# State space beside attention: softplus of all four channel parts ahead of the products, two parts at a time, and the rows of B and C in a pool of their own

## The chip, the core and the metric

The kernel runs on one core of a Trainium2 chip. Five engines with their own instruction queues work beside each other: TensorE (PE in the profile, its weight loads are PEld), VectorE (DVE), ScalarE (ACT), GpSimd (POOL) and SyncE (SP), which here issues nearly all DMAs. Each engine takes its instructions in the order of its queue, and waits at the first whose inputs or buffers are not ready, whatever stands behind it. The metric is the device time of one execution in microseconds, the median of the runs.

## What is computed

One sequence of four sublayers over `x` of shape (2, 1024, 256), each with a residual: attention with 16 heads of 128 and ALiBi, a ternary-quantized feed-forward layer, a selective state space (Mamba) layer, and a feed-forward layer that keeps two of four. The change is in the third:

```python
xz = einsum('bld,ed->ble', hidden_states, in_proj_weight);  x, z = split(xz)
x_conv = silu(sum(xp[:, w:w+l, :] * conv1d_weight[:, w] for w in range(4)))
x_dbl = einsum('bld,ed->ble', x_conv, x_proj_weight)   # dt_low (128), B (16), C (16)
delta = softplus(einsum('blr,dr->bld', dt_low, dt_proj_weight) + dt_proj_bias)
deltaA = exp(einsum('bld,dn->lbdn', delta, A))          # A = -exp(A_log)
dBu = einsum('bld,bln,bld->lbdn', delta, Bm, x_conv)
h = deltaA * h + dBu;  y = einsum('bdn,bn->bd', h, c)   # a scan over l
y = (y + x_conv * D) * silu(z);  out = einsum('bld,ed->ble', y, out_proj_weight)
```

There are 512 channels, held as four channel parts of 128 partitions, and 16 states: 64 pairs (part c, state n), called products below. `delta` is the softplus that the change moves. All is float32 here.

## The kernel before

The 2 x 1024 positions are cut into four chunks of 512: chunk 0 and 1 are the halves of the first sequence, 2 and 3 those of the second. Attention of a chunk is 16 heads of four tiles (128 queries each); a head of a second half sees 1024 keys and costs more than one of a first half. The loop at the end of the program runs attention of chunk k = 1, 2, 3 as a generator, and beside it, as another generator `rest(k-1)`, the other three sublayers of the chunk before. The first chunk's attention runs ahead of it, with the quantization of weights, and `rest(3)` runs alone at the end, the tail.

How the two are interleaved is written out: after each attention tile, `rest` is advanced until the sum of what it yielded has reached its share of `cost(k)`. A product yields 2.2 units, a softplus step 3. So a yield decides beside which attention tile, and so where in each engine's queue, the instructions behind it stand. Scans also carry an order against attention's row sums (`pace["front"]`, L756).

`state_space(k)` has a front and the products. **Front:** layernorm; input projection (L608); convolution on DVE (L624, L626); silu; the low-rank part `dtl` (matmul L639, copied to SBUF); softplus of part 0 by `steps(0)`; then B and C (`bcp` matmul, L648), stored to DRAM (L658), from where every product loads its row, broadcast to 128 partitions.

`steps(c)` (L544 to L575) is softplus of one part, 512 wide: a matmul into a PSUM bank of `ps_r` (L547, `dt`); on ACT Abs (L555, `se`), Relu (L556, `sv`), Exp (L561) and Ln (L563, `dl`); on DVE a correction `sr` (L568, L569); on POOL `dl` + `sr` (L570), plus `sv` (L572; on DVE where `short`, that is for chunk 1), and times `xs` (L574, `du`). `sv` and `se` have one buffer, `dl` and `du` two. steps(1), steps(2), steps(3) stand in the middle of the products of the part before, after product 16c - 8.

**Products.** Each of the 64 runs through stages with lags, in a software pipeline: ask for the rows of B and C (`bs`, `cs`, L691, SP's DMA queue, rings of 5 and 4 buffers), `db` = `du` x B (L736, POOL), `da` = exp(A x `dl`) (L750, ACT, into a bank of `ps_r`, of which there are two), the scan `hs` (L757, DVE), keep the last column (L766, DVE), `hc` = `hs` x C (L771, POOL), and the sum over n as transposes added in PSUM (`y`, L701, PE). At the end of a part the gate (L786 to L793). In the tail `db` comes from PE and ACT, and the buffers are more.

Attention, beside this, has scores on PE (`s`, L362), mask, ALiBi and row minimum on DVE (L366, L372), the exponential on ACT (L377), transposes on PE (`pt`, L293) copied to SBUF (`pT`, L296, ACT or DVE), `z` (L304, copied as `zs`, L309), the output product (`o`, L318) added to `x` on DVE (L324), and for the next head `pq`, `pk` (L335), `pv` (L342) on PE with their copies `qT`, `kT` (L338) and `v` (L347) on ACT, the last on ACT or DVE.

The memory pools matter too. The front's weights and activations (`mi`) are closed before the products' pool `m2` opens in their place, so the first row loads and buffers of `m2` wait until the front's last readers are done.

Of the kernel before, what the change touches and what calls it, by code (L numbers as in the profile page):

```python
# [9 lines left out]
F32 = mybir.dt.float32  # L10
BF16 = mybir.dt.bfloat16
F32R = mybir.dt.float32r
AF = mybir.ActivationFunctionType
ALU = mybir.AluOpType
# [3 lines left out]
P = 128  # L18
# [8 lines left out]
DI, DN, DR, DC = 512, 16, 128, 4  # L27
NDC = DI // P
NX = DR + 2 * DN
U = 512  # L30
# [11 lines left out]
def kernel(  # L42
# [21 lines left out]
    nc = tc.nc  # L64
# [6 lines left out]
    def bank(tag, bufs):  # L71
        return lambda name, dt=F32: ps.tile([P, 512], dt, tag=tag, name=name, bufs=bufs)
# [3 lines left out]
    ps_y, ps_r = bank("y", 1), bank("r", 2)  # L76
# [156 lines left out]
    for h in range(H):  # L233
# [10 lines left out]
    rows = a2.tile([H, S], F32, tag="alibi", name="rows", padded_shape=[P, S])  # L244
    nc.gpsimd.iota(
        rows, pattern=[[1, S]], base=0, channel_multiplier=0, allow_small_or_imprecise_dtypes=True,
# [179 lines left out]
    dt_bias = lambda c: cols_sb[:, c, DC + DN : DC + DN + 1]  # L426
# [90 lines left out]
    def state_space(k):  # L517
        b, u = CH[k]
        first, last, tail_end = u == 0, u == NU - 1, k == len(CH) - 1
        ps_da = ps_s if tail_end else ps_r  # L520

        short = not tail_end and CH[k + 1][1] == 0
        with ExitStack() as mctx:
            mc = mctx.enter_context(tc.tile_pool(name="mc", bufs=1, side="right"))
            dt_sb = mc.tile([P, DI], F32, name=f"dt_sb_{k}")
            out_sb = mc.tile([P, NDC, D], F32, name=f"out_sb_{k}")
            xs = mc.tile([P, NDC, U], F32, name=f"xs_{k}")
            sz = mc.tile([P, NDC, U], F32, name=f"sz_{k}")
            dtl = mc.tile([P, U], F32, name=f"dtls_{k}")
            work = lambda name: mc.tile([P, U], F32, tag="cv", name=name, bufs=2)  # L530
            diag = mc.tile([P, DN, UT, P], F32, name=f"diag_{k}") if tail_end else None
            one = mc.tile([P, 1], F32, name=f"one_{k}")
# [8 lines left out]
            marks = []  # L541
            paced = not tail_end

            def steps(c):  # L544

                vp = ps_r(f"dt_{k}_{c}")
                ended["by"] = nc.tensor.matmul(  # L547
                    vp, lhsT=dt_sb[:, c * P : (c + 1) * P], rhs=dtl, start=True, stop=True
                )


                v = row_of("sv", f"sv_{k}_{c}", 1)
                e = row_of("se", f"se_{k}_{c}", 1)
                with tc.issue_after(marks[0].ins):
                    nc.scalar.activation(e, vp, AF.Abs, bias=dt_bias(c))  # L555
                relu = lambda: nc.scalar.activation(v, vp, AF.Relu, bias=dt_bias(c))  # L556

                idle = tail_end and c == 0
                if not idle:
                    relu()  # L560
                nc.scalar.activation(e, e, AF.Exp, scale=-1.0)  # L561
                l = row_of("dl", f"dl_{k}_{c}", 2)
                log = nc.scalar.activation(l, e, AF.Ln, bias=one)  # L563
                if idle:
                    with tc.issue_after(log.ins):
                        relu()
                r = work(f"sr_{k}_{c}")
                nc.vector.tensor_scalar(r, e, 1.0, -1.0, ALU.add, ALU.add)  # L568
                marks.append(nc.vector.tensor_tensor(r, e, r, ALU.subtract))  # L569
                (nc.vector if idle else nc.gpsimd).tensor_tensor(l, l, r, ALU.add)  # L570
                dl = l
                (nc.vector if short or idle else nc.gpsimd).tensor_tensor(dl, v, l, ALU.add)  # L572
                du = row_of("du", f"du_{k}_{c}", 2)
                marks.append((nc.vector if idle else nc.gpsimd).tensor_tensor(du, dl, xs[:, c, :], ALU.mult))  # L574
                return dl, du  # L575

            def turned(c, du):

                tp = ps_r(f"dup_{k}_{c}")
                for t in range(UT):  # L580
                    nc.tensor.transpose(
                        tp[:, t * P : (t + 1) * P], du[:, t * P : (t + 1) * P], ident
                    )
                duT = row_of("duT", f"duT_{k}_{c}", 2)
                nc.scalar.copy(duT, tp)
                return duT


            with ExitStack() as ictx:

                mi = (mctx if tail_end else ictx).enter_context(tc.tile_pool(name="mi", bufs=1, side="right"))
                if tail_end:
                    in_sb = carried["in"]
                else:
                    in_sb = mi.tile([P, KC, 2 * DI], F32, name=f"in_sb_{k}")
                    nc.sync.dma_start(out=in_sb, in_=inT.rearrange("(c p) m -> p c m", p=P))
                xp_sb = mi.tile([P, NDC, NX], F32, name=f"xp_sb_{k}")
                nc.sync.dma_start(out=xp_sb, in_=xpT.rearrange("(c p) m -> p c m", p=P))
                nc.sync.dma_start(out=dt_sb, in_=dtT)
                nc.sync.dma_start(out=out_sb, in_=outT.rearrange("(c p) m -> p c m", p=P))  # L600
# [37 lines left out]
                for c in range(NDC):  # L638
                    nc.tensor.matmul(  # L639
                        dl_ps, lhsT=xp_sb[:, c, :DR], rhs=xs[:, c, :],  # L640
                        start=(c == 0), stop=(c == NDC - 1),
                    )
                nc.any.tensor_copy(dtl, dl_ps)
                parts, turns = {0: steps(0)}, {}
                yield 3
                bc_ps = ps_da(f"bcp_{k}")
                for c in range(NDC):
                    last_bc = nc.tensor.matmul(  # L648
                        bc_ps[: 2 * DN, :], lhsT=xp_sb[:, c, DR:], rhs=xs[:, c, :],
                        start=(c == 0), stop=(c == NDC - 1),  # L650
                    )
                if tail_end:
                    ended["by"] = last_bc
                    fill_in()
                bc = mi.tile([2 * DN, U], F32, name=f"bc_{k}", padded_shape=[P, U])
                nc.any.tensor_copy(bc, bc_ps[: 2 * DN, :])

                nc.sync.dma_start(out=bcd.rearrange("a n t -> (a n) t"), in_=bc)  # L658
                if tail_end:
# [7 lines left out]
                    bT = mc.tile([P, UT, DN], F32, name=f"bTs_{k}")  # L667
                    nc.vector.tensor_copy(bT, bT_ps[:, :, :DN])
                yield 4

            m2 = mctx.enter_context(tc.tile_pool(name="m2", bufs=1, side="right"))
            part = lambda tag, name, bufs: m2.tile([P, U], F32, tag=tag, name=name, bufs=bufs)
# [12 lines left out]
            def row(rows, a, tag, bufs):  # L685
                def ask(i):
                    c, n = prods[i]
                    if a == 0 and by_tensor(i):
                        return
                    rows[i] = part(tag, f"{tag}_{k}_{c}_{n}", bufs)  # L690
                    nc.sync.dma_start(  # L691
                        out=rows[i], in_=bcd[a, n : n + 1, :].to_broadcast([P, U])
                    )
                return ask
# [105 lines left out]
            for i in range(-5, len(prods) + DRAIN(k)):  # L800
                for lag, f in stages:
                    if 0 <= i - lag < len(prods):
                        f(i - lag)
                if i >= 0:
                    yield 2.2
                if 0 <= i < len(prods) and i // DN + 1 < NDC:
                    c = i // DN + 1
                    if i % DN == (DN // 4 if tail_end else DN // 2):
                        parts[c] = steps(c)
                        yield 3  # L810
                    if tail_end and i % DN == DN - 5:
                        turns[c] = turned(c, parts[c][1])
            for t in range(UT):
                op = (spare(k) if t % 2 else ps_r)(f"mo_{k}_{t}")
                for c in range(NDC):
                    ended["by"] = nc.tensor.matmul(  # L816
                        op[:, :D], lhsT=xs[:, c, t * P : (t + 1) * P], rhs=out_sb[:, c, :],
                        start=(c == 0), stop=(c == NDC - 1),
# [151 lines left out]
    for k in range(1, len(CH)):  # L970
        r, done = rest(k - 1), 0.0
# [76 lines left out]
```

## Time and profile before

| | us |
|---|---|
| median of 3 runs | 1836.29 (1833.47, 1836.29, 1837.93) |
| span of the profiled execution | 1836.9 |
| first `db` to last `hc`, chunk 0 | 348.47 to 566.27 |
| the same, chunk 1 | 824.43 to 1004.93 |
| the same, chunk 2 | 1237.73 to 1454.35 |

The profiled execution's own time is its span; it lies 0.6 us from the median. Times in the profile are microseconds from the start of the span. A window's row gives the busy time of each engine with the number of instructions, then TensorE's granted clock as a share of full speed, the DMA engines' busy share and GB/s. In a timeline a row gives start, duration, engine, line, operation, names and shape; the bracket holds the time the engine sat idle before it and what ended that. In a groups' row the figures behind the bar are busy time and mean ns, then idle time before the group by what ended it. Line numbers are those of the kernel before.

### The profile page before, as it was taken

The numbers are of one execution on the slowest core, as the hardware profiler recorded it, in microseconds if no ns is written. First come the engines' busy times: TensorE is split into PE (matmuls) and PEld (weight loads), VectorE is DVE, ScalarE is ACT, GpSimd is POOL, SyncE is SP. The second block draws the span as 40 slices with busy tenths as digits, with TensorE's granted clock in tenths as the row PEclk, the third lists the DMA queues.
The fourth block names the chain that finished last, engine by engine and source line by source line (L and its number), as shares of the span: only waits on it lengthen the run. The fifth ranks groups of instructions, "written<-read, shape, count | busy, mean of one in ns | idle before, by whom it ended". The sixth has DMA issues, their size and how long they took to land. (4 is left out here: it accounts for less than half of the span.)

```text
span 1836.9 us, 24217 instructions
## 1 busy us (share of the span) xinstructions
PE 1718.3 (94%) x7956; PEld 1144.2 (62%) x7956; DVE 1218.3 (66%) x2349; ACT 963.7 (52%) x1789; POOL 832.2 (45%) x674
## 2 busy tenths in 40 slices
PE   7999999998999999998888999999999999998899
PEld 4666666555656557755555667756656565566895
DVE  5666555777785473458886565557788655667975
ACT  3444474656563553555554545566555446446742
POOL 3324032588892000419998000418898500035870
PEclk9999999999999999999999999999999999999999
DMA  6443512466662311337787324227665430212541
GB/s 201 128 142 128 193 46 88 149 203 204 216 202 91 103 52 48 125 109 232 245 247 224 116 71 141 82 67 228 226 214 184 142 115 26 75 53 86 178 136 57
DMA packets 178301, 255.99 MB, mean 139 GB/s; under 512 B 16240, under 2 KB 90992, under 8 KB 177152
## 3 DMA queue, kind: packets, MB, share of 16 engines
q1 hardware_dynamic: 176752, 241.61, 41.4%
q0 software_dynamic: 1152, 12.58, 1.9%
q8 instruction: 63, 1.03, 0.2%
q14 instruction: 62, 0.51, 0.1%
q10 hardware_dynamic: 272, 0.26, 0.0%
HBM read 232.04 MB, written 22.35 MB: 138 GB/s over the span
## 5 line engine op out<-in xcount | busy, mean ns | idle before, releaser
L771 POOL TENSOR_TENSOR hc<-hs,cs 128x512 f32<-128x512 f32 x256 | 362.1, 1428 | 10.8 <-DVE ss L366 3.1
L362 PE MATMUL s<-kT,qT 128*128 128x512 f32 (+3 forms) x768 | 302.7, 495 | 19.9 <-DVE ss L366 18.0
L377 ACT ACTIVATE ss<-ss,nm 128x128 f32<-128x128 f32 (+7 forms) x256 | 198.8, 776 | 183.5 <-DVE nm L372 174.1
L366 DVE SCALAR_TENSOR_TENSOR ss<-s,lower 128x512 f32<-128x512 f32 (+3 forms) x384 | 204.6, 549 | 121.0 <-PE s L362 119.4
L736 POOL TENSOR_TENSOR db<-du,bs 128x512 f32<-128x512 f32 x192 | 259.2, 1356 | 44.4 <-DVE hs L757 30.6
L304 PE MATMUL z<-pT,v 128*128 128x512 f32 (+3 forms) x768 | 264.5, 492 | 10.9 <-ACT pT L296 10.2
L372 DVE CUSTOM_DVE_ANT_0 ss<-ss,alibi 128x128 f32<-128x128 f32 (+7 forms) x256 | 241.3, 945 | 3.5
L750 ACT ACTIVATE da<-dl,a_neg 128x512 f32<-128x512 f32 x256 | 177.9, 698 | 115.6 <-DVE hs L757 90.6
L304 PEld LDWEIGHTS z<-pT,v 128*128 128x128 f32 x768 | 142.8, 190 | 145.1 <-issue 92.7
L296 ACT COPY pT<-pt 128x512 f32<-128x512 f32 (+3 forms) x321 | 145.4, 474 | 162.0 <-PE pt L293 160.4
L293 PE MATMUL pt<-ident,ss 128*128 128x128 f32 x1152 | 180.3, 279 | 32.1 <-DVE x L324 18.5
L293 PEld LDWEIGHTS pt<-ident,ss 128*128 128x128 f32 x1152 | 140.0, 142 | 94.7 <-DVE x L324 33.0
L362 PEld LDWEIGHTS s<-kT,qT 128*128 128x128 f32 x768 | 127.9, 193 | 84.1 <-issue 43.4
L757 DVE TENSOR_TENSOR_SCAN hs<-da,db 128x512 f32<-128x512 f32 x128 | 153.8, 1210 | 38.6 <-ACT da L750 20.8
L757 DVE TENSOR_TENSOR_SCAN hs<-da,carry,db 128x512 f32<-128x512 f32 x128 | 159.1, 1269 | 24.4 <-POOL hc L771 14.7
L324 DVE SCALAR_TENSOR_TENSOR x<-o,rr,x 128x256 f32<-128x256 f32 x256 | 108.9, 476 | 76.7 <-PE o L318 76.5
L701 PE MATMUL y<-ident,hc 128*128 128x128 f32 x1024 | 144.8, 279 | 8.4 <-POOL hc L771 8.4
L342 PEld LDWEIGHTS pv<-wv,xT_a 128*128 128x128 f32 x1024 | 124.4, 192 | 37.1 <-issue 25.3
L342 PE MATMUL pv<-wv,xT_a 128*128 128x128 f32 x1024 | 125.8, 275 | 5.5 <-ACT zs L309 3.4
L701 PEld LDWEIGHTS y<-ident,hc 128*128 128x128 f32 x1024 | 121.0, 145 | 14.3 <-POOL hc L771 11.9
L318 PE MATMUL o<-wo,zs 128*128 128x256 f32 x512 | 125.4, 386 | 4.1 <-ACT kT L338 3.0
L335 PE MATMUL pq<-xT_a,wq 128*128 128x512 f32 x256 | 122.7, 601 | 0.7 <-ACT xT_a L148 0.7
(204 smaller groups left out, 2468.7 us busy)
## 6 DMA issues: line engine op xcount, KB each, us to landing
cs<-bcd SPq DMA_DIRECT2D x256, 256.0 KB, 3.8
bs<-bcd SPq DMA_DIRECT2D x192, 256.0 KB, 4.3
alibi<-alibi_d SPq DMA_DIRECT2D x32, 512.0 KB, 4.2
wq<-in_wqT_dram SPq DMA_DIRECT2D x64, 128.0 KB, 3.5
wk<-in_wkT_dram SPq DMA_DIRECT2D x64, 128.0 KB, 3.1
wv<-in_wvT_dram SPq DMA_DIRECT2D x64, 128.0 KB, 2.8
wo<-in_woT_dram SPq DMA_DIRECT2D x64, 128.0 KB, 2.8
alibi<-alibi_d SPq DMA_DIRECT2D x32, 256.0 KB, 3.6
```

Source lines behind the costliest of these rows:

```text
L293: nc.tensor.transpose(tp[:, i, :], s[:, (kb0 + i) * P : (kb0 + i + 1) * P], ident)
L304: nc.tensor.matmul(zp[:, q0:], lhsT=st["v_all"][:, kb, :], rhs=st["pts"][kb // 4][:, kb % 4, q0:], start=(kb == 0), stop=(kb == last),)
L342: nc.tensor.matmul(vp[:, t, :], lhsT=xT[:, c, t * P : (t + 1) * P], rhs=st["v"][:, c, :], start=(c == 0), stop=(c == KC - 1),)
L362: nc.tensor.matmul(sp[:, :n], lhsT=st["qT"][:, j * P : (j + 1) * P], rhs=st["kT"][:, k0 : k0 + n], start=True, stop=True,)
L366: nc.vector.scalar_tensor_tensor(s[:, k0 : k0 + n], sp[:, :n], CLIP, lower[:, S - W + k0 : S - W + k0 + n], op0=ALU.min, op1=ALU.max,)
L372: pace["tile"] = nc.vector.tensor_tensor_reduce(out=s[:, :W], in0=s[:, :W], in1=st["alibi"][:, :W], scale=1.0, scalar=3.0e38, op0=ALU.add, ...
L377: nc.scalar.activation(s[:, :W], s[:, :W], AF.Exp, bias=nm, scale=-1.0, accum_out=st["rs"][:, j : j + 1])
L701: nc.tensor.matmul(yTs[c][:, t * P : (t + 1) * P], lhsT=h[:, t * P : (t + 1) * P], rhs=ident, is_transpose=True, start=start and t == 0, s ...
L736: nc.gpsimd.tensor_tensor(db[i], du, brow.pop(i), ALU.mult)
L750: nc.scalar.activation(da[i], parts[c][0], AF.Exp, scale=a_neg[:, c, n : n + 1])
L757: nc.vector.tensor_tensor_scan(out=hs[i], data0=da.pop(i), data1=db.pop(i), initial=0.0 if first else carry[:, n, c : c + 1], op0=ALU.mult ...
L771: nc.gpsimd.tensor_tensor(hc[i], hs.pop(i), crow.pop(i), ALU.mult)
```

## The change

For chunks 0, 1 and 2 the softplus of all four parts is taken in the front, after B and C are stored and ahead of the products, by a new function `steps_of(pool, a)`: the same operations as `steps`, on two parts at once. The matmul, Abs and Relu stay one part each (a PSUM bank holds 512), Exp, Ln, the correction and the POOL operations take tiles of 2 x 512. It is called for parts 0 and 1 and then for parts 2 and 3; each time a pool `st` with one buffer of `sv`, `se` and `sr` is opened in the same memory, and each call yields 6 units. The results `dls`, `dus` hold all four parts. The mid-product steps and their yields of 3 are left to the tail, which is otherwise as before. `cost` is not changed: 9 units leave the products and the front has 9 more.

The memory is laid out anew: the rows of B and C have a pool `rings` that is open from the front on, instead of a place in `m2`; `dt_sb`, `dtl`, `xp_sb` and `bc` move to a pool `mw` that is closed before the products; `mi` is closed before the softplus. The `bcp` matmul and the store of B and C now come ahead of the softplus.

```diff
--- before.py
+++ after.py
@@ -522,11 +522,9 @@
         short = not tail_end and CH[k + 1][1] == 0
         with ExitStack() as mctx:
             mc = mctx.enter_context(tc.tile_pool(name="mc", bufs=1, side="right"))
-            dt_sb = mc.tile([P, DI], F32, name=f"dt_sb_{k}")
             out_sb = mc.tile([P, NDC, D], F32, name=f"out_sb_{k}")
             xs = mc.tile([P, NDC, U], F32, name=f"xs_{k}")
             sz = mc.tile([P, NDC, U], F32, name=f"sz_{k}")
-            dtl = mc.tile([P, U], F32, name=f"dtls_{k}")
             work = lambda name: mc.tile([P, U], F32, tag="cv", name=name, bufs=2)
             diag = mc.tile([P, DN, UT, P], F32, name=f"diag_{k}") if tail_end else None
             one = mc.tile([P, 1], F32, name=f"one_{k}")
@@ -574,6 +572,34 @@
                 marks.append((nc.vector if idle else nc.gpsimd).tensor_tensor(du, dl, xs[:, c, :], ALU.mult))
                 return dl, du
 
+            dls = None if tail_end else mc.tile([P, NDC, U], F32, name=f"dl_{k}")
+            dus = None if tail_end else mc.tile([P, NDC, U], F32, name=f"du_{k}")
+
+            def steps_of(pool, a):
+
+                cs = slice(a, a + 2)
+                v, e, r = (
+                    pool.tile([P, 2, U], F32, tag=t, name=f"{t}_{k}_{a}") for t in ("sv", "se", "sr")
+                )
+                for i in range(2):
+                    vp = ps_r(f"dt_{k}_{a + i}")
+                    nc.tensor.matmul(
+                        vp, lhsT=dt_sb[:, (a + i) * P : (a + i + 1) * P], rhs=dtl, start=True, stop=True
+                    )
+                    with tc.issue_after(marks[0].ins):
+                        nc.scalar.activation(e[:, i, :], vp, AF.Abs, bias=dt_bias(a + i))
+                    nc.scalar.activation(v[:, i, :], vp, AF.Relu, bias=dt_bias(a + i))
+                nc.scalar.activation(e, e, AF.Exp, scale=-1.0)
+                l = dls[:, cs, :]
+                nc.scalar.activation(l, e, AF.Ln, bias=one)
+                nc.vector.tensor_scalar(r, e, 1.0, -1.0, ALU.add, ALU.add)
+                nc.vector.tensor_tensor(r, e, r, ALU.subtract)
+                nc.gpsimd.tensor_tensor(l, l, r, ALU.add)
+                (nc.vector if short else nc.gpsimd).tensor_tensor(l, v, l, ALU.add)
+                nc.gpsimd.tensor_tensor(dus[:, cs, :], l, xs[:, cs, :], ALU.mult)
+                for c in range(a, a + 2):
+                    parts[c] = dls[:, c, :], dus[:, c, :]
+
             def turned(c, du):
 
                 tp = ps_r(f"dup_{k}_{c}")
@@ -586,15 +612,19 @@
                 return duT
 
 
-            with ExitStack() as ictx:
-
+            rings = mctx.enter_context(tc.tile_pool(name="rings", bufs=1, side="right"))
+            with ExitStack() as wctx, ExitStack() as ictx:
+
+                mw = (mctx if tail_end else wctx).enter_context(tc.tile_pool(name="mw", bufs=1, side="right"))
+                dt_sb = mw.tile([P, DI], F32, name=f"dt_sb_{k}")
+                dtl = mw.tile([P, U], F32, name=f"dtls_{k}")
                 mi = (mctx if tail_end else ictx).enter_context(tc.tile_pool(name="mi", bufs=1, side="right"))
                 if tail_end:
                     in_sb = carried["in"]
                 else:
                     in_sb = mi.tile([P, KC, 2 * DI], F32, name=f"in_sb_{k}")
                     nc.sync.dma_start(out=in_sb, in_=inT.rearrange("(c p) m -> p c m", p=P))
-                xp_sb = mi.tile([P, NDC, NX], F32, name=f"xp_sb_{k}")
+                xp_sb = mw.tile([P, NDC, NX], F32, name=f"xp_sb_{k}")
                 nc.sync.dma_start(out=xp_sb, in_=xpT.rearrange("(c p) m -> p c m", p=P))
                 nc.sync.dma_start(out=dt_sb, in_=dtT)
                 nc.sync.dma_start(out=out_sb, in_=outT.rearrange("(c p) m -> p c m", p=P))
@@ -641,8 +671,10 @@
                         start=(c == 0), stop=(c == NDC - 1),
                     )
                 nc.any.tensor_copy(dtl, dl_ps)
-                parts, turns = {0: steps(0)}, {}
-                yield 3
+                parts, turns = {}, {}
+                if tail_end:
+                    parts[0] = steps(0)
+                    yield 3
                 bc_ps = ps_da(f"bcp_{k}")
                 for c in range(NDC):
                     last_bc = nc.tensor.matmul(
@@ -652,7 +684,7 @@
                 if tail_end:
                     ended["by"] = last_bc
                     fill_in()
-                bc = mi.tile([2 * DN, U], F32, name=f"bc_{k}", padded_shape=[P, U])
+                bc = mw.tile([2 * DN, U], F32, name=f"bc_{k}", padded_shape=[P, U])
                 nc.any.tensor_copy(bc, bc_ps[: 2 * DN, :])
 
                 nc.sync.dma_start(out=bcd.rearrange("a n t -> (a n) t"), in_=bc)
@@ -667,6 +699,12 @@
                     bT = mc.tile([P, UT, DN], F32, name=f"bTs_{k}")
                     nc.vector.tensor_copy(bT, bT_ps[:, :, :DN])
                 yield 4
+                if not tail_end:
+                    ictx.close()
+                    for a in range(0, NDC, 2):
+                        with tc.tile_pool(name="st", bufs=1, side="right") as st:
+                            steps_of(st, a)
+                        yield 6
 
             m2 = mctx.enter_context(tc.tile_pool(name="m2", bufs=1, side="right"))
             part = lambda tag, name, bufs: m2.tile([P, U], F32, tag=tag, name=name, bufs=bufs)
@@ -687,7 +725,7 @@
                     c, n = prods[i]
                     if a == 0 and by_tensor(i):
                         return
-                    rows[i] = part(tag, f"{tag}_{k}_{c}_{n}", bufs)
+                    rows[i] = rings.tile([P, U], F32, tag=tag, name=f"{tag}_{k}_{c}_{n}", bufs=bufs)
                     nc.sync.dma_start(
                         out=rows[i], in_=bcd[a, n : n + 1, :].to_broadcast([P, U])
                     )
@@ -805,7 +843,7 @@
                     yield 2.2
                 if 0 <= i < len(prods) and i // DN + 1 < NDC:
                     c = i // DN + 1
-                    if i % DN == (DN // 4 if tail_end else DN // 2):
+                    if tail_end and i % DN == DN // 4:
                         parts[c] = steps(c)
                         yield 3
                     if tail_end and i % DN == DN - 5:
```

In the changed program, as built, the order of all engines' instructions outside the three product stages is the same as before. Within them the first scans stand one to two attention tiles later, behind the `sr` of both pairs: in chunk 0 scans 0.0 and 0.1 come in tile 1 of head 4 and scans 0.2 to 0.10 one after the other in its tile 2; by tile 0 of head 5 the scans stand where they stood before. In chunk 1 thirteen scans, 0.0 to 0.12, stand in tile 3 of head 4; before, the first stood in tile 3 of head 3. POOL's order has the three operations of pair 1, the three of pair 2 and then the products.

## The prediction

> **What bounds the kernel now.** I read the page's shares and slices first, then windows over the stages, the waits, and the timeline around one mid-product step.
>
> ```profile
> PE 1718.3 (94%) x7956; PEld 1144.2 (62%) x7956; DVE 1218.3 (66%) x2349; ACT 963.7 (52%) x1789; POOL 832.2 (45%) x674
> POOL 3324032588892000419998000418898500035870
> ```
>
> TensorE is busy 94% of the span, but POOL works in three blocks (the stages that hold the products of chunks 0, 1, 2) and in the tail. The windows give those stages, with a stretch between the first two for comparison:
>
> ```profile
> core 0: us, PE busy (x) PEld busy (x) DVE busy (x) ACT busy (x) POOL busy (x), PEclk, DMA share, GB/s
> 345.00:568.00 223.00, 204.63 (x987) 134.35 (x985) 178.54 (x313) 129.16 (x235) 193.31 (x138) 1.00 0.66 208
> 568.00:780.00 212.00, 209.03 (x898) 136.94 (x897) 105.81 (x234) 102.23 (x177) 24.06 (x21) 1.00 0.24 79
> 824.00:1005.00 181.00, 147.34 (x737) 104.73 (x736) 147.80 (x212) 96.07 (x198) 174.81 (x134) 0.93 0.78 241
> 1234.00:1456.00 222.00, 204.45 (x987) 134.24 (x985) 176.96 (x312) 129.14 (x235) 193.35 (x138) 1.00 0.65 209
> ```
>
> PE idles 3.0 us between the stages, but 18.4, 33.7 and 17.6 in the three product stages. Chunks 0 and 2 are PE-bound with POOL at 87%; chunk 1 (the short attention beside it) is POOL-bound: 174.81 of 181, 97%. A mid-product step looks like this in the timeline of chunk 0:
>
> ```profile
> 442.12 1.49 DVE L568 TENSOR_SCALAR sr<-se 128x512 f32<-128x512 f32 x1
> 443.93 0.68 DVE L569 TENSOR_TENSOR sr<-se,sr 128x512 f32<-128x512 f32 x1
> 444.75 1.27 POOL L570 TENSOR_TENSOR dl<-dl,sr 128x512 f32<-128x512 f32 x1 [1.42 <-DVE sr L569]
> 445.05 0.33 PE L293 MATMUL pt<-ident,ss 128*128 128x128 f32 x1 [1.62 <-DVE x L324]
> 451.74 1.56 PE L362 MATMUL s<-kT,qT 128*128 128x512 f32 x4 [1.25 <-DVE ss L366]
> 455.96 1.12 PE L362 MATMUL s<-kT,qT 128*128 128x512 f32 x2 [0.92 <-DVE ss L366]
> ```
>
> DVE's `sr` stands ahead of attention's `x` (L324), and PE waits 1.62; POOL, stepped three operations back, gives two more gaps, 3.79 in all. A head without a step has gaps of 0.73. So a step costs PE about 3.1 us; three per stage are 9.3.
>
> **The change, part by part.** Sums are against the profiled execution's span, 1836.9; the runs' median is 1836.3, so no correction.
>
> *Removed.* In each of chunks 0 to 2 three mid-product steps: 9.3 us of PE in chunks 0 and 2 each. Bounds: the 1.62 gap alone (4.9 a stage) to the whole 4.5 of a head pair with a step (13.5). In chunk 1 PE is not the bound; what is taken out of the products is POOL's 6 operations there, 7.7 us.
>
> *The same work, earlier and wider.* Abs and Relu stay 512 wide. Exp and Ln become 1024 wide: 1.15 against 2 x 0.63 and 2 x 0.72, by this row:
>
> ```profile
> L377 ACT ACTIVATE ss<-ss,nm 128x1024 f32<-128x1024 f32 x32 | 36.9, 1152 | 21.6 <-DVE nm L372 21.1
> ```
>
> That saves 0.4 of ACT per pair; ACT is at 53 to 58%, so nothing. POOL's 1024-wide form is not in the trace: twice 1.27 is 2.54; less the whole cost of its 128x3 copy (0.3) it is 2.24. I take 2.5: the long rows of the same operation are nearest. DVE's `sr` pair 0.47 + 0.68 becomes about 2.2 unhindered.
>
> *The chain ahead of the first product, chunk 0.* In the built program, pair 1 opens with its two dt matmuls split: the second stands on PE behind the z matmuls (5.75) and pq, pk, pv (1.88, 1.88, 1.95) of a head. PE: dt of part 0 ends 343.8, z 349.5, projections 354.9 with a little slack, dt of part 1 355.8. ACT: Abs, Relu, Exp end 358.3, Ln 359.5; DVE's `sr` 361.8. POOL's first add cannot start before. Three operations x 2.5: the second ends 366.9, the third 369.4. Pair 2 uses the same buffers (`st`, one buffer each), so its first Abs waits for the second add, which reads `sv`: 366.9. On ACT, attention's softmax exponential (L377) and pT copies are queued behind that Abs from about 362.5, and PE's pt and z behind them. Four Abs and Relu to 369.4, Exp 370.4, `sr` 373.5, three POOL operations: 381.1. There the first `db` (L736) starts, by POOL's order; before it started at
>
> ```profile
> 348.47 3.72 POOL L736 TENSOR_TENSOR db<-du,bs 128x512 f32<-128x512 f32 x3 [1.65 <-DMA bs<-bcd]
> ```
>
> so 33 us later. The row and wait for the bs load goes: the row buffers are a pool of their own now and their loads (SP) and the bcd store ahead of them lie before the softplus; nothing on SP waits longer.
>
> *What is late next.* Products are laid out against attention's tiles, and the scans stand in DVE's order, the decays in ACT's. The change adds 9 units of pacing to the front, takes 9 out of the products, and its first scans land one or two tiles later. In the built program nine scans (0.2 to 0.10) stand in a row on DVE ahead of attention's next `x`; on ACT the copies zs, qT, kT, v stand behind decays whose bank those scans free (two banks). Then PE's projections and pt wait on POOL. That such queueing reaches across is seen in the kernel before, a scan held by a decay that stood behind a v copy:
>
> ```profile
> 382.11 1.22 DVE L757 TENSOR_TENSOR_SCAN hs<-da,db 128x512 f32<-128x512 f32 x1 [9.37 <-ACT da L750]
> ```
>
> Scan 0.10 needs `db` 0.10, the 17th POOL operation from the first: 381.1 + 17 x 1.27 = 402.7, with 1.3 for contention with DVE 404.0; scan 1.2, decay 0.7, v copy 0.6: 406.6. PE's pt of head 4 stands behind it; before it ran at 384.94. So +21.8; +1.6 for three `y` groups that were already done by then, -2.6 for dt matmuls and `y` opening already done in the new order: **+20.7**. Bounds: 17 (POOL at 2.24, no contention) to 26 (17 operations at the stage's mean 1.44 and ACT released late). Gaps of this length lower the clock, as in chunk 1:
>
> ```profile
> 855.00:863.00 8.00, 4.64 (x20) 3.49 (x21) 5.97 (x8) 2.52 (x5) 8.00 (x7) 0.79 1.00 294
> 858.60 0.85 PE L701 MATMUL y<-ident,hc 128*128 128x128 f32 x4 [3.01 <-POOL hc L771]
> ```
>
> Clock 0.79 over 8 us is a loss of about 1.7; I add 2 per stage (0 to 5). After the burst the products are where they were in tile order. Chunk 0: 20.7 - 9.3 + 2 = **+13.4** (bounds 17 - 13.5 = +3.5, and 26 - 4.9 + 5 = +26). Chunk 2 has the same rows: **+13.4**.
>
> *Chunk 1*, POOL-bound. Same chain from 826.8 (dt of part 1 ends), `sr` 832.6, POOL 835.1, DVE's second add (DVE here, 1.36 to 1.73) 836.5, third 839.1; pair 2's Abs to 839.1, `sr` 842.4, POOL 844.9, DVE 846.3, POOL 848.8: first `db`, before 824.43. From there 128 products' operations without a break at 1.27 (unhindered) or 1.347 (the stage's mean):
>
> ```profile
> L736 POOL TENSOR_TENSOR db<-du,bs 128x512 f32<-128x512 f32 x64 | 86.1, 1351 | 5.4 <-DMA bs<-bcd 5.4
> L771 POOL TENSOR_TENSOR hc<-hs,cs 128x512 f32<-128x512 f32 x64 | 85.4, 1339 | 2.7 <-DMA cs<-bcd 2.7
> ```
>
> 162.6 to 172.4, so the end is at 1011.4 to 1021.2 against 1004.9: +6.5 to +16; **+11.6**, nearer the mean, whose DVE neighbours stay. The 24.4 that POOL starts later is paid with the 7.7 it no longer does and its former waits of 8.1.
>
> Sum: 13.4 + 11.6 + 13.4 = +38.4, **1875**. The tail (chunk 3) keeps its own steps.
>
> **Two rules of the skill.** The Trainium skill, "Perfetto Trace Analysis", section "Optimizing Scalar/DVE Operations", says that grouping into larger operations helps a saturated engine, while on engines that are not saturated but cause bubbles elsewhere, breaking up lets work complete sooner. ACT and DVE here are at 53 to 82%, so the rule speaks against pairs; by it the sum stays a loss, and single parts would start the products earlier. "TensorE: Matmul & The Clock Gate", section "Part 1: The HAM clock gate", puts halving after one idle window of about 3.4 us; at that figure one hole would cost an estimated 1.7 to 3.4, against the 2 taken.
>
> **The rivals.** *A, faster: the front is covered.* If attention has other work for ACT and DVE until the products come, only the removed steps count: -9.3 twice, and in chunk 1 none to -9.3: 1818 to 1809. For it: PE gaps of the mid steps are plain; POOL is at 87%, with room. Against it: the static orders. It decides where `db` 0.10 ends by about 379 (the v copy before at 381), that is, a first `db` by 357.5; I reach 381.1, and even with POOL operations free the pair chain gives 366. *B, no change:* holes as long as the gaps removed (9.3 each) and chunk 1 held by its idle 8.1; 1837. *C, small loss:* chunks 0 and 2 come out at their lower bounds, chunk 1 at +6.5 to +11.6: 1842 to 1855. *D, larger loss:* chunks 0 and 2 become POOL-bound as chunk 1 is: 381.1 + 128 x 1.445 + the 24.5 that POOL idles there for DVE and rows = 590.6 against 566.3: +24 each, with chunk 1 at +16: 1901. For it: POOL would be at 89% in a stage grown by 13; against: its idle need not stay.
>
> **How the numbers follow.** Main case (1855 to 1890) 0.50; C 0.15; D (above 1890) 0.16; B 0.05; A 0.14. A change of 0.3% (5.5 us) is about what a measurement can tell from none: faster 0.14, same 0.05, slower 0.81. The range leaves out A, most of B, and D's far end: 1841 to 1902.
>
> **What the profile after would show.** First `db` near 381 (chunk 0), 849 (chunk 1); in the page's row for 512-wide `db` the idle before it for SP's rows gone; PE gaps of 5 to 20 us in chunk 0 between 362 and 407, ended by POOL or by copies on ACT; no 1.6 gap at a step later; clock below 1.00 in that window; POOL above 97% in chunk 1 after its first `db`; the span between stages unchanged (212). I am wrong if ACT's queue clears before the burst, if POOL's wide form costs much less than 2.24, or if the tiles after the burst run faster than before by more than 9.3.

## The result, and the profile after

The changed kernel takes 1909.1 us (median of 4 runs, 1896.4 to 1915.2) against 1837.1: a ratio of 1.038, 95% interval 1.034 to 1.042. It is slower, as forecast, but by 72 us where 38 were forecast, and outside the range of 1841 to 1902. A second set of runs of the same kernel gave 1902.1 (1899.9 to 1906.6), 1.035 (1.033 to 1.038). The profiled execution is the shortest of its set, span 1894.6, so 57.7 of the loss can be read in it, and the rest is a matter of how executions differ (experiment 12).

The page of the changed kernel:

```profile
PE 1736.2 (92%) x7956; PEld 1156.2 (61%) x7956; DVE 1207.2 (64%) x2344; ACT 958.4 (51%) x1768; POOL 815.6 (43%) x658
POOL 3333040396973000408999000408789600034970
```

TensorE issues the same 7956 matmuls and is busy 17.9 us longer: the same work at a lower clock (mean granted clock 0.977, before 0.989). The other 39.8 us of the loss is TensorE idle.

Where it is lost can be read from attention, which runs in the same order in both kernels: I take the start of DVE's row minimum (L372) of each head's first tile, and compare head lengths. Chunk 0 ends 22.5 us behind, chunk 1 adds 12.9, chunk 2 adds 20.9, the tail 1.4; between the product stages nothing moves but head 1 of chunks 1 and 2 (+1.5 and -2.7). In chunk 0, head by head, in us against before:

| head | 3 | 4 | 5 | 6 | 7 | 8 | 9 | 10 | heads 5 to 10 |
|---|---|---|---|---|---|---|---|---|---|
| changed kernel | +3.1 | +15.3 | +1.1 | -0.3 | +4.4 | -0.9 | +0.6 | -0.5 | +4.4 |

Heads 3 and 4 are the forecast hole. Its chain on the timeline of the changed kernel (start, duration, then idle before and what ended it):

```profile
365.76 0.69 ACT L590 ACTIVATE se<-dt,cols_sb 128x512 f32<-128x512 f32 x1 [4.71 <-POOL dl L598]
...
372.46 1.12 PE L362 MATMUL s<-kT,qT 128*128 128x512 f32 x2 [3.42 <-DVE ss L366]
...
379.73 7.01 POOL L774 TENSOR_TENSOR db<-du,bs 128x512 f32<-128x512 f32 x5
...
392.88 1.22 DVE L795 TENSOR_TENSOR_SCAN hs<-da,db 128x512 f32<-128x512 f32 x1 [1.03 <-POOL db L774]
...
392.96 3.78 PE L342 MATMUL pv<-wv,xT_a 128*128 128x128 f32 x16 [6.94 <-ACT zs L309]
...
397.86 2.08 PE L318 MATMUL o<-wo,zs 128*128 128x256 f32 x4 [1.12 <-ACT qT L338]
...
401.53 2.07 PE L318 MATMUL o<-wo,zs 128*128 128x256 f32 x4 [1.60 <-ACT kT L338]
...
403.97 1.33 PE L293 MATMUL pt<-ident,ss 128*128 128x128 f32 x5 [0.37 <-ACT v L347]
```

Pair 2's Abs waits for POOL's second add, the first `db` starts at 379.73, and the copies zs, qT, kT, v come out of ACT one by one behind decays whose scans wait for POOL's `db`. PE's projection (pv) takes 3.78 instead of 1.95: it runs at half the clock. The windows of the changed kernel show that, and something that was not forecast, behind it:

```profile
core 0: us, PE busy (x) PEld busy (x) DVE busy (x) ACT busy (x) POOL busy (x), PEclk, DMA share, GB/s
380.00:407.00 27.00, 16.97 (x55) 11.59 (x55) 18.75 (x31) 11.39 (x18) 27.00 (x22) 0.70 0.61 189
440.00:470.00 30.00, 26.35 (x133) 17.76 (x132) 18.29 (x35) 15.22 (x30) 16.02 (x12) 1.00 0.46 137
470.00:500.00 30.00, 26.31 (x113) 16.21 (x114) 24.28 (x44) 14.93 (x28) 30.00 (x23) 0.94 0.75 231
```

POOL, which had been the late one, is idle for 14 of the 30 us from 440, and then busy without a break from 470. In the timeline it is one wait of 13.56 us; the longest of its kind in chunk 0 before was 5.9. The scan that frees a `db` buffer stands on DVE behind attention's scores (L366), for which DVE waits 11.68 us while PE is at z and the projections of a head, and behind the gate of part 0 (L831), which follows them without a pause. After it TensorE waits for POOL and for a copy:

```profile
456.61 0.59 ACT L824 COPY ysb<-y 128x512 f32<-128x512 f32 x1
...
457.20 1.20 DVE L366 SCALAR_TENSOR_TENSOR ss<-s,lower 128x512 f32<-128x512 f32 x2 [11.68 <-PE s L362]
...
458.32 0.68 DVE L831 TENSOR_TENSOR xs<-yb,sz 128x512 f32<-128x512 f32 x1
...
458.92 1.21 DVE L795 TENSOR_TENSOR_SCAN hs<-da,db 128x512 f32<-128x512 f32 x1
...
460.21 2.04 POOL L774 TENSOR_TENSOR db<-du,bs 128x512 f32<-128x512 f32 x1 [13.56 <-DVE hs L795]
...
475.41 0.66 PE L739 MATMUL y<-ident,hc 128*128 128x128 f32 x4 [1.92 <-POOL hc L809]
...
489.20 2.05 PE L342 MATMUL pv<-wv,xT_a 128*128 128x128 f32 x16 [1.27 <-DVE zs L309]
```

The mid-product steps, which stood in heads 4, 6 and 8, are gone with their gaps. In their place stand these.

### The profile page after: what moved, and what is told of

It reads as the page before. It is cut to its first block, busy times and chain, and to the rows that moved or that the text cites. A ratio compares the mean times of both kernels' runs of the same rounds, so it can differ in the third digit from the quotient of the medians.

```text
span 1894.6 us, 24222 instructions
## 1 busy us (share of the span) xinstructions
PE 1736.2 (92%) x7956; PEld 1156.2 (61%) x7956; DVE 1207.2 (64%) x2344; ACT 958.4 (51%) x1768; POOL 815.6 (43%) x658
## 5 line engine op out<-in xcount | busy, mean ns | idle before, releaser
L809 POOL TENSOR_TENSOR hc<-hs,cs 128x512 f32<-128x512 f32 x256 | 338.7, 1341 | 34.6 <-PE y L739 20.8
L366 DVE SCALAR_TENSOR_TENSOR ss<-s,lower 128x512 f32<-128x512 f32 (+3 forms) x384 | 203.0, 546 | 224.3 <-PE s L362 222.8
L304 PE MATMUL z<-pT,v 128*128 128x512 f32 (+3 forms) x768 | 270.6, 501 | 23.2 <-ACT pT L296 22.6
L774 POOL TENSOR_TENSOR db<-du,bs 128x512 f32<-128x512 f32 x192 | 263.9, 1386 | 44.2 <-DVE hs L795 40.6
L372 DVE CUSTOM_DVE_ANT_0 ss<-ss,alibi 128x128 f32<-128x128 f32 (+7 forms) x256 | 240.1, 940 | 3.8
L296 ACT COPY pT<-pt 128x512 f32<-128x512 f32 (+3 forms) x313 | 141.2, 473 | 148.1 <-PE pt L293 146.3
L293 PEld LDWEIGHTS pt<-ident,ss 128*128 128x128 f32 x1152 | 139.7, 143 | 89.1 <-issue 28.1
L342 PEld LDWEIGHTS pv<-wv,xT_a 128*128 128x128 f32 x1024 | 128.9, 198 | 54.6 <-issue 22.7
L342 PE MATMUL pv<-wv,xT_a 128*128 128x128 f32 x1024 | 131.1, 283 | 21.7 <-ACT zs L309 17.0
L739 PEld LDWEIGHTS y<-ident,hc 128*128 128x128 f32 x1024 | 121.1, 145 | 12.3 <-POOL hc L809 10.6
```

The source lines that it names most:

```text
L293: nc.tensor.transpose(tp[:, i, :], s[:, (kb0 + i) * P : (kb0 + i + 1) * P], ident)
L304: nc.tensor.matmul(zp[:, q0:], lhsT=st["v_all"][:, kb, :], rhs=st["pts"][kb // 4][:, kb % 4, q0:], start=(kb == 0), stop=(kb == last),)
L342: nc.tensor.matmul(vp[:, t, :], lhsT=xT[:, c, t * P : (t + 1) * P], rhs=st["v"][:, c, :], start=(c == 0), stop=(c == KC - 1),)
L366: nc.vector.scalar_tensor_tensor(s[:, k0 : k0 + n], sp[:, :n], CLIP, lower[:, S - W + k0 : S - W + k0 + n], op0=ALU.min, op1=ALU.max,)
L372: pace["tile"] = nc.vector.tensor_tensor_reduce(out=s[:, :W], in0=s[:, :W], in1=st["alibi"][:, :W], scale=1.0, scalar=3.0e38, op0=ALU.add, ...
L739: nc.tensor.matmul(yTs[c][:, t * P : (t + 1) * P], lhsT=h[:, t * P : (t + 1) * P], rhs=ident, is_transpose=True, start=start and t == 0, s ...
```

## Theories

A, the prediction's: the loss is the hole, and the steps taken out give 9.3 us a stage back, less only if they were worth less. B, the rival: the order of the products behind the hole is another one, and it costs what the steps gave. The steps' yields of 3 units were taken out of the middle of each part with them. By the pacing's formula the whole of chunk 0 has 304.8 units on 64 tiles, 38.1 on eight tiles, that is on two heads; a part of 16 products yielded 16 x 2.2 + 3 = 38.2 before, and 35.2 now. So by the formula each part of the products stood against the same two-head pattern of attention in the kernel before, and in the changed one each part begins 0.6 tiles earlier in it than the last.

## Experiments

**1. What a mid-product step costs.** The kernel before, with parts 1 to 3 on part 0's delta:

```diff
-                        parts[c] = steps(c)
+                        parts[c] = steps(c) if tail_end else parts[0]
                         yield 3
```

> The kernel before, without the three mid-product softplus steps of chunks 0 to 2: parts 1 to 3 use the delta of part 0, so their softplus is left out; the yields stay, and the front is that of before. Prediction's step (a mid step costs PE 3.1 us): about 9 us less in each of chunks 0 and 2, up to 9 in chunk 1, so 1809 to 1818. Rival (the gaps belong to the dense heads of attention, whatever stands in them): under 3 us less per stage, 1829 to 1837.

Measured: 1826.8, ratio 0.993 (0.991 to 0.994), 12.8 us less, between the two expectations. Heads 3 to 10 of chunk 0 take 7.0 less: heads 6 and 8 are 2.9 and 3.0 us shorter, heads 5, 7 and 9 half a us longer. In chunk 2 the same heads take 5.5 less. Chunk 1 gains nothing (it is 2.3 longer), though POOL has 7.7 us less to do there. The three steps are worth 7.0 and 5.5 rather than 9.3, and neither expectation holds in chunk 1.

**2. Only the first pair in the front.** `range(0, 2, 2)` for `range(0, NDC, 2)`, parts 2 and 3 on the delta of parts 0 and 1, a yield of 12.

> The changed kernel with only the first pair's softplus in the front; parts 2 and 3 use the delta of parts 0 and 1 (their softplus is left out), the yields are the same 12. Prediction's steps: first db of chunk 0 near 369, the hole at heads 4 and 5 some 9 us instead of 18, and with 9 gained later chunk 0 stands near zero: 1837 to 1847. Rival (nothing comes back after the hole, since the products' order behind head 5 is that of the changed kernel): chunks 0 and 2 about +13 each, 1860 to 1870.

Measured: 1881.7, ratio 1.023 (1.020 to 1.027). The first `db` is at 369.8, as expected, and heads 3 and 4 lose 10.8. But heads 5 to 10 lose another 6.1, and chunk 1 loses 16. The total is beyond both expectations; heads 5 to 10 speak for B.

**3. Products three to four tiles later,** with 19 units more in the pacing's total.

```diff
-                        yield 6
+                        yield 6 if a == 0 else 25
```

> The changed kernel with 25 units yielded after the second pair instead of 6, and 19 more in the pacing's total: the products stand three to four attention tiles later, the softplus where it was. Prediction's steps: the first db stays near 380 in chunk 0, but no scan stands ahead of attention that POOL has not reached, so the hole goes (18 to under 4), and if the mid steps were worth 9 each the time is near 1830 to 1840. Rival (products squeezed towards the end of attention, nothing gained after the hole): 1855 to 1870.

Measured: 1864.3, ratio 1.014 (1.012 to 1.016). In chunk 0 heads 3 and 4 take 10.6 less than before, head 2, now denser with the front, 6 more: with the scans behind POOL's softplus there is no hole. Yet chunk 0 ends 7.0 behind, since the later heads lose. The hole is a matter of what stands in the queues ahead of attention, not of the softplus as such; and taking it away does not win the stage.

**4. One part at a time.** `steps_of` on one part, 512 wide, two buffers of each temporary.

> The changed kernel with softplus in the front one part at a time, 512 wide, two buffers of each temporary. If the width and the wait of the second pair for the first make the hole: the first db comes some 10 us earlier (near 368), the hole is near 8, 1850 to 1870. If any softplus of all four parts ahead of the products costs the same: within 5 us of the changed kernel.

Measured: 1888.6, ratio 1.027 (1.024 to 1.030), between the two expectations. First `db` 375.2, hole in heads 3 and 4 9.2, half of 18.4; heads 5 to 10 lose 7.7. The pairs' width and wait make half of the hole. The median is 13 to 20 us below the changed kernel's (two sets of runs), so some of that reaches the total, while chunk 1 loses 20.8 here instead of 12.9.

**5. The order alone.** As experiment 1, with the yields of the changed kernel. They stand ahead of the `bcp` matmul here, so the rows of B and C come later too:

```diff
-                parts, turns = {0: steps(0)}, {}
-                yield 3
+                parts, turns = {0: steps(0)}, {}
+                yield 3 if tail_end else 12
...
-                        parts[c] = steps(c)
-                        yield 3
+                        parts[c] = steps(c) if tail_end else parts[0]
+                        if tail_end:
+                            yield 3
```

> As e1 (no mid steps, parts 1 to 3 use the delta of part 0), but 9 more units yielded in the front and none mid-product, so that from head 5 on the products stand against attention's tiles just as in the changed kernel, with the front's softplus short as before. If the order behind the hole is what costs the changed kernel the gain of the mid steps: heads 5 to 10 of chunk 0 take about 4 us more than before instead of 5 less, some 9 us per stage more than e1: 1840 to 1855. If instead POOL being late after the hole costs it: within 4 of e1, 1823 to 1831.

Measured: 1862.1, ratio 1.013 (1.011 to 1.016): 35 us above experiment 1, which does the same work. In chunks 0 and 2 the scans stand at the same attention tiles as in the changed kernel from the tenth on; in chunk 1 they do not. In chunk 0 there is hardly a hole (heads 3 and 4 together +1.7), and heads 5 to 10 lose 7.1. In the timeline of this kernel the signature of the changed one returns, the same POOL wait to the hundredth and the same waits of PE:

```profile
366.25 6.15 POOL L736 TENSOR_TENSOR db<-du,bs 128x512 f32<-128x512 f32 x5 [18.40 <-DMA bs<-bcd]
...
445.94 2.04 POOL L736 TENSOR_TENSOR db<-du,bs 128x512 f32<-128x512 f32 x1 [13.56 <-DVE hs L757]
...
461.14 0.66 PE L701 MATMUL y<-ident,hc 128*128 128x128 f32 x4 [1.91 <-POOL hc L771]
...
474.20 0.68 DVE L309 COPY zs<-z 128x512 f32<-128x512 f32 x1
...
474.94 3.48 PE L342 MATMUL pv<-wv,xT_a 128*128 128x128 f32 x16 [2.98 <-DVE zs L309]
```

What the eye should follow: POOL is starved as in the changed kernel; then a row of scans stands on DVE ahead of the copy zs, the last of them each waiting 1.2 us for its `db`, and PE waits for zs; then PE is at half the clock. No softplus of four parts in the front is needed for that, which speaks for B. POOL starts late in this kernel too, though: its first `db` waits 18.40 us for a row and comes at 366.25, against 349.04 in experiment 1. What a late POOL does without the new order is left to experiment 8.

**6. The memory layout alone.** The new pools and the `bcp` matmul ahead of the softplus, with the steps of the kernel before (`parts[0] = steps(0)` in place of the two calls, `dt_sb` and `dtl` in the pool `rings`).

> The changed kernel's memory layout (rows of B and C in a pool of their own, weights of the front in a pool that is closed, B and C computed ahead of the softplus) with the softplus steps of the kernel before, one part in the front and three mid-product. Every theory: within 4 us of before (1833 to 1843); the first db's wait for its row (1.65 us in chunk 0, 3.1 in chunk 1) goes. If the layout itself were part of the loss it would be 5 or more slower.

Measured: 1848.8, ratio 1.006 (1.004 to 1.009): 10 us slower, as the lesser expectation had it. Head 3 takes 3.4 longer in chunk 0 and 4.3 in chunk 2, and nothing comes back. The `bcp` matmul (3.6 us of PE) filled the time between part 0's dt matmul and the next tile; now it stands ahead of dt, the first `db` comes at 351.68 rather than 348.47, and attention's copies wait once behind scans, with a half-clock window after it:

```profile
358.07 1.13 PE L318 MATMUL o<-wo,zs 128*128 128x256 f32 x4 [1.19 <-ACT kT L338]
...
360.11 1.06 PE L293 MATMUL pt<-ident,ss 128*128 128x128 f32 x4 [0.92 <-DVE v L347]
```

Row loads are no longer waited for at the first `db`, and it did not matter. The pools were not separated from the place of `bcp`.

**7. Two buffers of the temporaries.**

```diff
-                    for a in range(0, NDC, 2):
-                        with tc.tile_pool(name="st", bufs=1, side="right") as st:
-                            steps_of(st, a)
-                        yield 6
+                    with tc.tile_pool(name="st", bufs=2, side="right") as st:
+                        for a in range(0, NDC, 2):
+                            steps_of(st, a)
+                            yield 6
```

> The changed kernel with two buffers of the temporaries in the front, so that the second pair's first Abs does not wait for POOL's second add of the first pair (4.7 us on ACT in chunk 0). Prediction's chain: first db some 4 us earlier, the hole in chunks 0 and 2 smaller by 4 to 9 each, 1888 to 1902. If that wait was covered: within 5 us of the changed kernel's 1909.

Measured: 1907.2, ratio 1.038 (1.035 to 1.042), as the changed kernel. In chunk 0 heads 3 and 4 lose 13.0 instead of 18.4, 5.4 less as expected, though the first `db` is not earlier (379.4); heads 5 to 10 lose 6.0, and chunk 1 loses 26.0 instead of 12.9 (18.2 in the second profile, experiment 12). A hole mended locally, with no gain at the end.

**8. The old yields with the new front.** The changed kernel with 1.5 units yielded after each pair and 3 in the middle of each part, where nothing is computed any more.

> The changed kernel with the yields of the kernel before: 3 units in the front, 3 in the middle of each part (nothing else stands there). From head 5 on the products then stand against attention's tiles as in e1; ahead of it thirteen scans instead of eleven stand before the next head's transposes. If the order behind the hole is the second half of the loss: heads 5 to 10 of chunk 0 take about 5 us less than before instead of 4.4 more; the hole grows by up to 5; 1880 to 1900. If POOL's late start itself spoils those heads: they stay at +4 or worse, 1905 or more.

Measured: 1908.0, ratio 1.039 (1.037 to 1.041). Both halves of the mechanism at once: heads 5 to 10 take 3.8 less than before instead of 4.4 more, but heads 3 and 4 lose 28.3 instead of 18.4, as thirteen scans now stand ahead of attention's `x` instead of eleven:

```profile
387.77 2.34 PE L739 MATMUL y<-ident,hc 128*128 128x128 f32 x8 [8.78 <-POOL hc L809]
...
406.66 1.11 PE L293 MATMUL pt<-ident,ss 128*128 128x128 f32 x4 [3.37 <-DVE v L347]
...
423.32 2.08 PE L362 MATMUL s<-kT,qT 128*128 128x512 f32 x2 [5.47 <-DVE ss L366]
```

The expectation of the total missed (1880 to 1900): the hole grew by 9.9 and not by up to 5. With experiments 1 and 5 this is a square, for chunk 0 in us against before:

| | heads 3 and 4 | heads 5 to 10 |
|---|---|---|
| short front, old order (1) | -2.2 | -4.8 |
| short front, new order (5) | +1.7 | +7.1 |
| all softplus in front, old order (8) | +28.3 | -3.8 |
| all softplus in front, new order (changed kernel) | +18.4 | +4.4 |

The order sets the second column: heads 5 to 10 lose with the new order and gain with the old one, even in experiment 8, where POOL's first `db` starts at 380.35, as late as in the changed kernel. So a late POOL is not what costs there, and B holds for these heads. The first column is mainly the front's, but the order moves it too, by 3.9 one way and 9.9 the other. Chunk 2 repeats the pattern (second column -4.8, +9.1, -4.7, +4.5). Chunk 1 does not (+1.8, +10.0, +7.3, -2.2), and with the long front its hole is 14.4 to 14.5 with either order. In the total the old order gains the long front nothing: 1908.0 against 1902 to 1909.

**9. zs always on ACT.** `nc.scalar.copy` for `nc.any.tensor_copy` in `values`.

> The changed kernel with the copy of z (zs) always on ACT, where it is free to go to DVE in the others; the order of scans is unchanged. If zs standing on DVE behind six scans is what costs head 7 of chunks 0 and 2 its 4 to 6 us: head 7 gains 3 or more, 1895 to 1904. If the scans' place alone matters, whichever engine copies: within 4 us of the changed kernel's 1907 to 1909.

Measured: 1901.4, ratio 1.036 (1.031 to 1.040), not apart from the changed kernel's 1902 to 1909; the total would fit the first expectation too, and the head decides. Head 7 of chunk 0 gains nothing (+6.8, against +4.4). On ACT the copy stands behind the decays of the same scans, and PE waits 3.43 for it, against 1.27 in the changed kernel:

```profile
491.82 0.69 ACT L788 ACTIVATE da<-dl,a_neg 128x512 f32<-128x512 f32 x1 [1.75 <-DVE carry L804]
...
492.45 0.58 ACT L309 COPY zs<-z 128x512 f32<-128x512 f32 x1
...
493.08 3.78 PE L342 MATMUL pv<-wv,xT_a 128*128 128x128 f32 x16 [3.43 <-ACT zs L309]
```

Moving the copy to the other engine does not take it out from behind the scans.

**10. Late and even.** The changed kernel with 3 and 20 units in the front and 2.63 per product (not the 4.34 of the expectation), the total raised to fit. A part of 16 products then takes 7.8 tiles by the formula.

> The changed kernel with 3 and 20 units yielded in the front and 4.34 per product, so that a part of 16 products takes eight attention tiles again and the first scans stand behind POOL's softplus. If hole and order make up the loss: no gap above 3 us in heads 3 to 5, heads 5 to 10 near zero or below; 1832 to 1850. If late products lose by themselves, as e3's later heads did: 1858 to 1870.

Measured: 1892.1, ratio 1.030 (1.028 to 1.031). A miss. There is no hole (heads 3 and 4 take 3.3 less), but head 2, into which the denser front falls, takes 9.0 more, heads 5 to 10 lose 3.8, and heads 11 to 14, with the feed-forward layer squeezed to the end, lose 7.5. Close to eight tiles a part is not enough by itself.

**11. The steps of the kernel before in six pieces,** issued with products 1, 2, 3, 5, 7 and 9 of a part, the 3 units yielded after product 8 as before.

> The kernel before with each mid-product step of chunks 0 to 2 cut in six pieces, issued with products 1, 2, 3, 5, 7 and 9 of a part, the 3 units still yielded after product 8; the products' order is that of e1. If what a mid step costs (7 us a stage in chunk 0, by e1) is its being one run of instructions ahead of attention's: most of it comes back, 1827 to 1834. If it is the work itself: 1836 to 1842.

Measured: 1859.9, ratio 1.012 (1.010 to 1.014). A miss: heads 6 and 8 are 1.8 shorter, as hoped for, but heads 3, 5 and 7 are 3.3 to 4.0 longer and chunk 1 loses 7.5. The order is not quite that of experiment 1, as the expectation had it: in heads 3, 5 and 7, the ones that lose, some scans stand one or two tiles later. Whether that is the whole cost was not taken apart. No version tried here that does all the work beats the kernel before.

**12. The changed kernel again.**

> The changed kernel once more. Its profiled execution (1896.4) was the shortest of four (1906 to 1915 the others, at granted clocks of 0.965 to 0.971 instead of 0.977). If the clock makes the difference: a profile at a clock near 0.970 takes 1905 to 1912, chunks 0 and 2 within 3 us of the first profile (22.7 and 23.6 over before) and chunk 1 some 20 to 25 over before instead of 12.9. If something else varies: the same clock with another time.

Measured: 1902.1 (1899.9 to 1906.6); profiled span 1898.1 at clock 0.972, so below the 1905 to 1912 expected near 0.970; chunk 1 lost 18.2, not 20 to 25. Most heads repeat the first profile within 0.2 us; the difference sits mainly in two places: head 5 of chunk 1 (+10.9 instead of +3.7) and head 4 of chunk 2 (+17.7 instead of +15.3). These windows show the two profiles around head 5 of chunk 1, the first profile, then the second (columns as in the windows above):

```profile
855.00:905.00 50.00, 29.46 (x116) 19.33 (x115) 34.13 (x48) 24.20 (x47) 43.55 (x31) 0.81 0.51 155
```

```profile
853.00:903.00 50.00, 29.30 (x113) 18.93 (x111) 34.12 (x42) 21.96 (x41) 43.45 (x32) 0.75 0.52 157
```

With the clock at 0.75 rather than 0.81, fewer instructions fit into the same 50 us. Over all eight executions of this kernel times run from 1896 at 0.977 to 1915 at 0.968 and 1912 at 0.965: mostly the lower the clock, the longer, though not in strict order. That the clock is the cause of the spread and not its sign is argued, not shown.

## Why the prediction was wrong

- *The chain ahead of the first product*: right. First `db` forecast at 381.1, measured 379.73; pair 2's Abs forecast to wait until 366.9, measured 365.76. Chunk 1's first `db` comes at 871.74, which is 849.2 without the 22.5 lost before, against 848.8. POOL's wide form took 2.34 to 2.50 in ten of sixteen cases and 2.73 to 3.22 in six, against 2.5 taken.
- *The hole*, forecast 20.7 and 2 for the clock: heads 3 and 4 lost 18.4. The mechanism (scans in a row ahead of attention's copies, decays ahead of them on ACT) is the one in the timeline. Experiment 6 lost 3.4 there with the new layout and the moved `bcp` matmul, which the prediction gave no price at all; how much of that is in the 18.4 was not shown.
- *Removed, 9.3 us in chunks 0 and 2*: this step failed. Taken out alone the steps are worth 7.0 in chunk 0 (experiment 1), inside the bounds of 4.9 to 13.5. But the sentence "After the burst the products are where they were in tile order" is false: the scans agree with those before at tile 0 of head 5, stand up to two tiles later or earlier through heads 5 to 9, and agree again only near the end of head 9, as the yields had gone with the steps. The order costs 11.9 us in heads 5 to 10 (experiment 5 against 1), or 8.2 with the long front (changed kernel against experiment 8). So instead of -9.3 these heads gave +4.4: some 14 us a stage, in two stages, more than the 19 by which the profile exceeds the forecast; the smaller hole gives part of it back. This is the term that failed, not the whole loss: with the old order kept (experiment 8) these heads gave -3.8, but the hole grew by 9.9.
- *Chunk 1*: +11.6 forecast; 12.9 in the first profile, 18.2 in the second. The size is near, the reasoning is not: it took chunk 1 for POOL-bound, and experiment 1 took 7.7 us of POOL work out of it without a gain, POOL's idle rising from 5.7 to 16.8 over its products. In the changed kernel POOL is 96% busy there from its first `db` to its last `hc`, and 92% in the second profile, where above 97% was forecast. What adds up to chunk 1's loss behind its hole stays open.
- *The clock*: 2 us a stage was too little. TensorE's half-rate windows add up to 41.4 us in the profile before and to 89.1 and 107.2 in the two after; the same matmuls are busy for 17.9 and 18.5 us longer, some 7, 3 and 6 of it in the three stages of the first. In the hole alone one window of 17 us is at half rate; the hole with its clock still stayed under the 22.7 forecast.
- *The medians*: the forecast was made against one execution, and the kernel's executions became less alike: 1833 to 1840 before, 1896 to 1915 after. 13 of the 72 us lie between the first profile and the median of its set.
- *Sums*: two were off without moving the forecast. 406.6 less 384.94 is 21.7, not 21.8, and the terms of rival C give 1850 to 1855, not 1842 to 1855.
- *Rules weighed*: breaking up the work instead of grouping it ("Perfetto Trace Analysis", section "Optimizing Scalar/DVE Operations", in the Trainium skill) pointed the right way: single parts (experiment 4) came out 13 to 20 us below the pairs, though they lost 49 against before. Six pieces instead of one step (experiment 11) cost 22.

## What to carry to other kernels

Where two streams are woven together by a pacing in units, an instruction group's yields are part of its effect: taking the group out moves everything behind it against the other stream, and here, with a short front, that alone was worth 35 us (experiment 5 against 1), more than the group itself (12.8); with the long front, putting the yields back gained nothing in the total (experiment 8). Ask of such a change first whether the period of one stream still fits the other, and compare the orders of the queues to the end of the stage, not to the first place where they agree again. A local repair of one gap (experiments 3, 7, 8) can be paid back in full a few heads later, so it is the length of the stage that decides.

## What the runs showed of the hardware

Half-rate windows of the matmul clock came in lengths of 3.41 us and multiples of it (6.83, 10.24, 13.65, 17.07), but for the one cut off by the end of the span. Most sat within a few us of a TensorE gap of 1.3 to 10.4 us, but not all: that at 797.2 in the first profile after has no gap above 0.92 near it. The first profile after, with 39.8 us more TensorE idle than before, has 47.7 us more at half rate. POOL's add or product of 128x1024 took 2.34 to 2.50 us in ten of sixteen cases of the first profile after, less than twice 1.27, and 2.73 to 3.22 in the other six. DVE was busy all through one of the short ones (2.36, at 371.95), so a busy DVE alone does not make the long ones; what does was not taken apart.
